# Two readers of a logits bank: the copies and the maxima of a key tile start at different heads

## The chip, the cores and the metric

The kernel runs on one core of a Trainium2 chip. The metric is the device time of one launch in microseconds (us). Before the change it is 3161.52 us, the median of three runs (3156.13 to 3167.02). The engines are named as in the profile: PE is TensorE, PEld its weight loads, DVE VectorE, ACT ScalarE, POOL GpSimd, SP the queue that issues DMAs.

## What is computed

Eight images of 512 channels and 32 x 32 pixels go through a convolutional block with two attention bottlenecks, and then through a grouped 1x1 convolution. Cut to what bears on the change, each of the two bottlenecks of an image does this:

```python
z = cbs(yi, m_cv1_w[i], m_cv1_bn[i], 1)                    # 3x3 convolution, SiLU
q, k, v = conv2d(z, qkv_w, 0) split in three, 4 heads of 64
logits = jnp.einsum('bhdi,bhdj->bhij', q, k + r) * HD ** (-0.5)
a = jax.nn.softmax(logits, axis=-1)                        # over 1024 keys
out = jnp.einsum('bhij,bhdj->bhdi', a, v)
ys.append(yi + silu(bn_eval(conv2d(out, m_cv2_w[i], 0))))
```

Around it stand a GroupNorm and a 1x1 convolution (cv1), a 1x1 convolution over all branches (cv2), and a second GroupNorm with the last layer's 1x1 convolution (l). Everything is float32.

## The kernel before

**Units of attention.** The attention is cut into 64 units, called passes here: image, bottleneck, pair of heads (hp) and half of the 1024 queries. A pass keeps its logits transposed: 128 keys on the partitions, 512 queries along the row, one bank of PSUM for each of the two heads. There are KT = 8 key tiles of 128 keys. The methods of `class Unit` (L493 to L585) are the steps:

- `logits(t)`, L502: two matmuls (L510) fill one bank for each head; ScalarE copies both banks into the SBUF tile `st` (L517); from the second tile on, VectorE keeps a running elementwise maximum `mx` of the tiles (L522). For t = 1 it takes the maximum of the first tile's copy and the second tile's bank, afterwards of `mx` and the bank. The first tile has no maximum.
- `top()` and `spread()`, L524 and L533: PE transposes `mx` (L530), VectorE reduces it to the negated maximum of each query (L531), and PE spreads that over the partitions into `mb` (L539).
- `soften(t)`, L542: VectorE adds `mb` to the logits (L544).
- `exponent(t)`, L546: ScalarE takes the exponential in place (L548); GpSimd adds the tiles up (L555).
- `values(t)`, L557: PE multiplies the exponentials with v into `po` (L562).
- `finish()` and `divide()`, L571 and L581: PE sums over the keys (L576), ScalarE copies the sum out (L579), VectorE takes reciprocals (L583) and multiplies (L585).

**The order.** The loop at L1047 to L1086 runs over the passes and, within a pass, over pairs of key tiles. While pass u is softened, exponentiated and multiplied with v, the logits of the next pass `nxt` are made. For each pair t, t + 1 it writes: `soften` of both; `exponent(t)` (not for t = 0); `values` of the two tiles before; for t = 0 `divide` of the pass before; `nxt.logits` of both tiles; the remaining exponentials. Then `advance` writes filler for PE: convolutions of other stages (cv1, cv2, 3x3 products at L313, the projection qkv, the last layer), with their evictions by ScalarE (L130 for SiLU, L396, L412, L333, L349) and by VectorE (L399, L430, L457, L486).

An engine carries out its instructions in the order in which the build queues them. That order is the program's as far as an instruction is ready in the build's own estimate; three chains fix it further. `act_turn` (L188) chains the copies and the exponentials on ScalarE, `in_turn` (L182) the maxima, the additions of soften and the steps of the 3x3 transform on VectorE, and `pe_turn` (L196) the attention's matmuls on PE. `divide` is in no chain. Semaphores between engines come from the tiles that an instruction reads and writes.

**PSUM.** All logits, fillers and small results take their banks in turn from one pool of five (`ps_f`, L63, tag `bank`); `mb` and `po` have pools of their own. A bank is written again only when both of its readers are done.

Of the kernel before, what the change touches and what calls it, by code (L numbers as in the profile page):

```python
# [17 lines left out]
ALU = mybir.AluOpType  # L18
# [21 lines left out]
def conv_preact_kernel(ctx: ExitStack, tc: tile.TileContext, x, cv1, cv2, mcv1, qkv, mcv2, bn, rw, rh, conv, s_in, t_in, out):  # L40
    nc = tc.nc
# [23 lines left out]
    def pair(p, tag, name):  # L65
        return p.tile([P, 2, HALF], F32, tag=tag, name=name)

    def bank(name):
        return ps_f.tile([P, HALF], F32, tag="bank", name=name)
# [112 lines left out]
    def in_turn(instruction):  # L182

        if turn:
            tc.add_manual_dep(instruction.ins, turn.pop().ins.name, IN_ORDER, reason="order of VectorE")
        turn.append(instruction)

    def act_turn(instruction):  # L188

        if act_last:  # L190
            tc.add_manual_dep(instruction.ins, act_last.pop().ins.name, IN_ORDER, reason="order of ScalarE")
        act_last.append(instruction)
# [3 lines left out]
    def pe_turn(instruction):  # L196

        if pe_last:
            tc.add_manual_dep(instruction.ins, pe_last.pop().ins.name, IN_ORDER, reason="order of TensorE")
        pe_last.append(instruction)  # L200
# [292 lines left out]
    class Unit:  # L493
# [8 lines left out]
        def logits(self, t):  # L502

            if t == 0:
                self.begin()
            lg = [bank(f"lg_{self.name}_{t}_{h}") for h in range(2)]
            for h in range(2):
                r = slice(HD * h, HD * h + HD)
                pe_turn(
                    nc.tensor.matmul(  # L510
                        lg[h], self.k[r, ts(t, P)], self.q[r, self.hp, ts(self.half, HALF)], start=True, stop=True
                    )
                )
            st = pair(stp, "st", f"st_{self.name}_{t}")
            self.st.append(st)
            for h in range(2):
                act_turn(nc.scalar.copy(st[:, h], lg[h]))  # L517
            if t == 1:
                self.mx = pair(one, "mx", f"mx_{self.name}")
            for h in range(2 if t else 0):  # L520
                so_far = self.st[0] if t == 1 else self.mx
                in_turn(nc.vector.tensor_tensor(self.mx[:, h], so_far[:, h], lg[h], ALU.max))  # L522

        def top(self):  # L524

# [625 lines left out]
```

## Time and profile before

| what | value |
|---|---|
| median of 3 runs | 3161.52 us |
| profiled execution, its own time | 3162.82 us |
| span of the profiled execution | 3161.1 us |
| granted clock of TensorE, mean | 0.996 |
| instructions in the span | 34185 |
| DMA | 399.35 MB, 126 GB/s in the mean |
| exponentials L548 on ScalarE | 512, mean 1068 ns |
| additions of soften L544 on VectorE | 512, mean 1215 ns |
| reciprocals L583 on VectorE | 128, mean 1723 ns |
| table loads on ScalarE (L130 and L548) | 223, 1283 ns each |

The profile shows one execution. A group of instructions is a line of the kernel with its engine, operation and tiles; behind it stand the number, the busy time in us, the mean duration of one in ns, and the idle time of the engine just before them with what ended most of it. The waits tell who waited for whom, in us, times and the longest. A wait for several semaphores is put down to the one that came last. In the timeline neighbouring instructions of one line are merged: the first number is the start of the first, the second the time to the end of the last, and a bracket gives the idle time of the engine before and its releaser. "issue" stands for time in which nothing that the profile shows was waited for; for weight loads, most of it is their spacing behind the matmuls.

Outside the attention stages lie the first 174 us (the first convolution and the making of weights) and the last 163 us. From 174 to 2998 us PE is busy for 2770.7 of 2824 us, VectorE for 1910.8 and ScalarE for 1630.7.

### The profile page before, as it was taken

Reading aid. Unit: us, or ns where it says so; the run is one execution under the profiler, and the core shown is the slowest. Engines: PE = TensorE matmul, PEld = TensorE weight load, DVE = VectorE, ACT = ScalarE, POOL = GpSimd, SP = SyncE. Lnnn points to the kernel's source line nnn. Section 1 sums busy time; section 2 is a strip of 40 time slices with the busy share of each in tenths; the row PEclk is TensorE's granted clock in tenths of the full one; section 3 lists DMA queues with packets and bytes.
Section 4 is the critical chain, followed back from the end, with each engine's and each line's share of the span. In section 5 each row is a group of like instructions: output and inputs, shape, how many; then the busy total and the mean of one; then the engine's idle time right before and its main releaser. Section 6 shows DMA issues by size and latency. Waiting matters only on the chain.

```text
span 3161.1 us, 34185 instructions
## 1 busy us (share of the span) xinstructions
PE 3077.0 (97%) x11668; PEld 1515.3 (48%) x11668; DVE 2049.9 (65%) x2718; ACT 1721.0 (54%) x2349; POOL 1398.4 (44%) x1867
## 2 busy tenths in 40 slices
PE   7999999998999999999999999999999999999999
PEld 3645354454445454455445454454445454453333
DVE  5446577567667576667666676767666676767642
ACT  3245765855655555644656455544656455546621
POOL 2104444546444554455444454445444464444520
PEclk9999999999999999999999999999999999999999
DMA  8852352421233232424233332424233332413356
GB/s 289 292 182 74 130 180 87 153 77 63 88 116 131 79 128 71 149 84 148 84 116 130 114 127 70 153 85 136 91 110 130 120 120 70 150 64 120 120 205 217
DMA packets 142014, 399.35 MB, mean 126 GB/s; under 512 B 13072, under 2 KB 14352, under 8 KB 141840
## 3 DMA queue, kind: packets, MB, share of 16 engines
q1 hardware_dynamic: 141120, 396.94, 36.6%
q8 instruction: 92, 1.51, 0.2%
q14 instruction: 82, 0.67, 0.1%
q10 hardware_dynamic: 720, 0.23, 0.0%
HBM read 317.42 MB, written 79.69 MB: 126 GB/s over the span
## 4 chain that ended last, share of the span: by engine, by line
PE 75%; DVE 4%; ACT 4%; issue 2%; DMA 1%; POOL 1%; SPq 0%; ACTq 0%; DVEq 0%; POOLq 0%
PE cv L175 15%; PE m L313 13%; PE po L562 12%; PE lg L510 12%; PE l L175 7%; PE qk L175 6%; PE v L405 3%; PE m L175 3%; PE den L576 2%; PE mb L539 2%; PE mt L530 1%; ACT st L517 1%; DVE st L544 1%; ACT st L548 1%; DVE mx L522 1%
## 5 line engine op out<-in xcount | busy, mean ns | idle before, releaser
L555 POOL TENSOR_TENSOR sum<-sum,st 128x256 f32<-128x256 f32 x1536 | 1132.0, 771 | 552.1 <-ACT st L548 547.7
L522 DVE TENSOR_TENSOR mx<-mx,lg 128x512 f32<-128x512 f32 x768 | 477.8, 682 | 417.6 <-ACT st L517 417.4
L517 ACT COPY st<-lg 128x512 f32<-128x512 f32 x1024 | 525.0, 597 | 356.1 <-PE lg L510 331.7
L548 ACT ACTIVATE st<-st 128x1024 f32<-128x1024 f32 x512 | 539.1, 1068 | 304.1 <-DVE st L544 302.9
L544 DVE TENSOR_TENSOR st<-st,mb 128x1024 f32<-128x1024 f32 x512 | 604.4, 1215 | 60.2 <-PE mb L539 60.2
L555 POOL TENSOR_TENSOR sum<-st,st 128x256 f32<-128x256 f32 x256 | 185.1, 754 | 788.8 <-ACT st L548 788.8
L313 PE MATMUL m<-plane,w_m 128*128 128x256 f32 x2304 | 528.8, 383 | 4.9 <-ACT cv2s L130 2.7
L562 PE MATMUL po<-st,v 128*64 128x512 f32 x2048 | 497.8, 605 | 18.2 <-ACT st L548 16.2
L510 PE MATMUL lg<-q,k 64*128 64x512 f32 x2048 | 510.9, 617 | 2.9 <-ACT y L130 2.9
L313 PEld LDWEIGHTS m<-plane,w_m 128*128 128x128 f32 x2304 | 426.4, 189 | 129.5 <-issue 45.1
L175 PE MATMUL cv<-y,w_cv 128*128 128x512 f32 x1024 | 464.5, 599 | 7.9 <-ACT cv2s L130 4.6
L510 PEld LDWEIGHTS lg<-q,k 64*128 64x128 f32 x2048 | 177.3, 186 | 328.2 <-issue 267.4
L175 PEld LDWEIGHTS cv<-y,w_cv 128*128 128x128 f32 x1024 | 185.8, 190 | 248.1 <-issue 226.4
L562 PEld LDWEIGHTS po<-st,v 128*64 128x64 f32 x2048 | 128.8, 136 | 323.6 <-issue 237.3
L175 PE MATMUL cv<-x,w_cv 128*128 128x512 f32 x512 | 237.0, 610 | 10.6 <-ACT y L130 3.7
L175 PE MATMUL l<-x,w_l 128*128 128x512 f32 x512 | 236.9, 606 | 7.9 <-DVE mx L522 6.9
L175 PE MATMUL qk<-z,w_qkv 128*128 128x512 f32 x512 | 234.0, 600 | 1.4 <-DVE mx L522 1.4
L583 DVE RECIPROCAL rb<-rb 128x256 f32<-128x256 f32 x128 | 215.5, 1723 | 26.0 <-ACT rb L579 25.8
L531 DVE TENSOR_REDUCE nm<-mt 128x4 f32<-128x512 f32 x128 | 82.3, 684 | 144.7 <-PE mt L530 144.7
L579 ACT COPY rb<-den 128x512 f32<-128x512 f32 x64 | 37.3, 583 | 230.4 <-PE den L576 230.4
L175 PEld LDWEIGHTS cv<-x,w_cv 128*128 128x128 f32 x512 | 95.3, 194 | 132.0 <-issue 109.3
L175 PEld LDWEIGHTS l<-x,w_l 128*128 128x128 f32 x512 | 93.4, 191 | 130.4 <-issue 112.2
(145 smaller groups left out, 2408.8 us busy)
## 6 DMA issues: line engine op xcount, KB each, us to landing
w_m<-w_m SPq DMA_DIRECT2D x96, 768.0 KB, 4.8
w_cv<-in_cv SPq DMA_DIRECT2D x90, 512.0 KB, 3.5
y<-y SPq DMA_DIRECT2D x64, 512.0 KB, 4.8
x<-in_x SPq DMA_DIRECT2D x56, 512.0 KB, 5.2
y<-y SPq DMA_DIRECT2D x64, 256.0 KB, 3.5
k<-r SPq DMA_DIRECT2D x32, 512.0 KB, 3.6
res<-y SPq DMA_DIRECT2D x32, 512.0 KB, 4.0
xr<-in_x SPq DMA_DIRECT2D x32, 512.0 KB, 4.1
```

The costliest lines, as they stand in the source:

```text
L175: nc.tensor.matmul(ps, w, moving, start=(n == 0), stop=(n == len(terms) - 1))
L313: nc.tensor.matmul(ps[:, ts(co, 256)].rearrange("p (t x) -> p t x", x=F), w[:, co, c, dx], u[:, 9 * c : 9 * c + 8, dx : dx + F], start=(j ...
L405: nc.tensor.matmul(ps[:, ts(j, P)], z[:, c, ts(4 * j4 + j, P)], w[:, c, 512 + P * hp : 512 + P * hp + P], start=(c == 0), stop=(c == IT - 1),)
L510: nc.tensor.matmul(lg[h], self.k[r, ts(t, P)], self.q[r, self.hp, ts(self.half, HALF)], start=True, stop=True)
L517: act_turn(nc.scalar.copy(st[:, h], lg[h]))
L522: in_turn(nc.vector.tensor_tensor(self.mx[:, h], so_far[:, h], lg[h], ALU.max))
L531: nc.vector.tensor_reduce(self.nm[:, h], mt, AX.X, ALU.max, negate=True)
L544: in_turn(nc.vector.tensor_tensor(st, st, flat(self.mb), ALU.add))
L548: act_turn(nc.scalar.activation(st, st, AF.Exp))
L555: nc.gpsimd.tensor_tensor(flat(self.acc)[:, part], flat(so_far)[:, part], st[:, part], ALU.add)
L562: nc.tensor.matmul(self.po[HD * h : HD * h + HD], self.v[:, t, ts(h, HD)], self.st[t][:, h], start=(t == 0), stop=(t == KT - 1),)
L583: nc.vector.reciprocal(self.rb[:, r], self.rb[:, r])
```

## The change

In `logits(t)` the two copies and the two maxima are written in another order. Before: copy of head 0, copy of head 1, maximum of head 0, maximum of head 1. After: copy of head 0, maximum of head 1, copy of head 1, maximum of head 0. Operands, shapes, numbers of instructions and the chains `act_turn` and `in_turn` are the same; within the chains the maxima of a tile change places. For t = 0 there is no maximum, and the two copies stay as they were.

```diff
             self.st.append(st)
-            for h in range(2):
-                act_turn(nc.scalar.copy(st[:, h], lg[h]))
             if t == 1:
                 self.mx = pair(one, "mx", f"mx_{self.name}")
-            for h in range(2 if t else 0):
-                so_far = self.st[0] if t == 1 else self.mx
-                in_turn(nc.vector.tensor_tensor(self.mx[:, h], so_far[:, h], lg[h], ALU.max))
+            so_far = self.st[0] if t == 1 else self.mx
+
+            def copy(h):
+                act_turn(nc.scalar.copy(st[:, h], lg[h]))
+
+            def greater(h):
+                if t:
+                    in_turn(nc.vector.tensor_tensor(self.mx[:, h], so_far[:, h], lg[h], ALU.max))
+
+            copy(0)
+            greater(1)
+            copy(1)
+            greater(0)
```

## The prediction

> **What bounds the kernel.** I first read the busy times of the page, then its costliest groups, the waits, and the timeline of single passes (one pass is one Unit: 64 passes of eight key tiles).
>
> ```profile
> PE 3077.0 (97%) x11668; PEld 1515.3 (48%) x11668; DVE 2049.9 (65%) x2718; ACT 1721.0 (54%) x2349; POOL 1398.4 (44%) x1867
> ```
>
> TensorE works in 97% of the 3161.1 us span, and the chain that ended last is 75% PE. So an edit pays only if it takes away a stretch in which PE stands still, and costs only if it makes one. VectorE (65%) and ScalarE (54%) have idle time in the mean; what counts is where they are late.
>
> ```profile
> L522 DVE TENSOR_TENSOR mx<-mx,lg 128x512 f32<-128x512 f32 x768 | 477.8, 682 | 417.6 <-ACT st L517 417.4
> L517 ACT COPY st<-lg 128x512 f32<-128x512 f32 x1024 | 525.0, 597 | 356.1 <-PE lg L510 331.7
> ```
>
> A maximum takes 682 ns, a copy 597 ns. VectorE is idle 417.6 us before its maxima, nearly all released by the copies. From the third key tile on, a maximum reads nothing that a copy writes; the two only read the same bank. So the program keeps two reads of one bank apart, in the order in which they are written: copy first, maximum second. The changed kernel will do the same in its own order: head 0 copy, then maximum; head 1 **maximum, then copy**. ScalarE will wait for VectorE, which this trace never shows.
>
> ```profile
> DVE mx L522 <- ACT st L517: 433.2, 174, 9.0
> PEld po L562 <- ACT st L548: 78.0, 92, 4.6
> PE po L562 <- ACT st L548: 16.2, 14, 3.7
> PE cv L175 <- DVE mx L522: 4.1, 5, 1.7
> ```
>
> The waits (us in total, times, longest): the big one is VectorE's and not PE's. PE's waits for a maximum that frees a bank are l 6.9 us, cv 4.1, po 2.0, m 1.6, mt 1.6 and qk 1.4: 17.6 us in 20 waits. PE also waits for the exponentials that feed values().
>
> **The change, part by part.** It adds and removes no instruction: 1024 copies, 896 maxima, the same DMAs. It turns round which engine reads head 1 first, in 448 key tiles (the first tile of a pass has no maximum).
>
> *Step 1, a pair of tiles with VectorE free.* In the pass whose third pair starts at 1220.41 us, the four copies run from 1221.64 to 1223.69 and the four maxima from 1222.26 to 1224.74. Maxima follow each other every 0.60 us, copies every 0.48; a maximum began 0.04 us after the copy it waited for. In the new order, maximum 1 runs beside copy 0, maximum 0 beside copy 1: two slots of 0.60 to 0.72 us a tile; from 1221.64 the maxima end near 1224.16, 0.58 earlier, and the copies and the exponential behind them 0.5 later. The second and the fourth bank are freed 0.58 earlier, the first and third at the old time. For PE this is worth at most 0.58 us in each of the 20 waits, and no more than the wait: l 3x0.58, cv 5x0.58, po 1.7, m 1.6, mt and qk 0.58 each: 9.1 us. Half of the banks gain nothing: I take **-5 us** (0 to -9). That VectorE is done sooner otherwise hides in its idle time.
>
> *Step 2, the second key tile of a pass.* This is the tile with the new wait. Behind spread() VectorE has two additions of soften (2.35 us together), two reciprocals (3.36) and two products (0.69) before it reaches the maxima; PE meanwhile needs about 5 us to the end of the logits. VectorE is late there by construction:
>
> ```profile
> 1241.44 2.35 DVE L544 TENSOR_TENSOR st<-st,mb 128x1024 f32<-128x1024 f32 x2 [0.95 <-PE mb L539]
> ...
> 1243.71 3.36 DVE L583 RECIPROCAL rb<-rb 128x256 f32<-128x256 f32 x2
> 1243.99 1.99 PE L510 MATMUL lg<-q,k 64*128 64x512 f32 x8
> 1245.21 2.05 ACT L517 COPY st<-lg 128x512 f32<-128x512 f32 x4 [2.20 <-PE lg L510]
> 1245.91 1.98 PE L175 MATMUL cv<-y,w_cv 128*128 128x512 f32 x4
> 1246.99 0.69 DVE L585 TENSOR_TENSOR q<-po,rb 128x256 f32<-128x256 f32 x2
> 1247.12 2.03 ACT L548 ACTIVATE st<-st 128x1024 f32<-128x1024 f32 x2
> 1247.59 1.28 DVE L522 TENSOR_TENSOR mx<-st,lg 128x512 f32<-128x512 f32 x2
> 1248.26 2.02 PE L562 MATMUL po<-st,v 128*64 128x512 f32 x8 [0.37 <-ACT st L548]
> ```
>
> (Columns: start, us from first start to last end, engine and line.) ScalarE does its four copies without a wait, the last from 1246.64, and goes on to the two exponentials, which PE's values() is already waiting for. In the changed kernel the last copy waits for maximum 1, which can't start before 1247.59: it ends 0.69 later, 1248.28, and the copy starts near 1248.32, **1.68 us late**. Behind it in ScalarE's queue stand exactly those exponentials, and behind them PE's values matmuls, then everything else on PE. This pass loses 1.7 us.
>
> I did this subtraction for the second tile of each of the 63 passes after the first, from the timeline: (start of the first maximum + 0.73) - (start of the last copy), less ScalarE's idle time before the exponential. The exponentials become late by 100 us in all, 1.6 in the mean. What covers it is PE's filler between the logits and values(): the time by which an exponential is done before its values matmul. In **17 passes** there is none (0.05 to 0.1 us, as above): delays of 0.35 to 1.7, sum 24.7 us. In **9 more** the delay exceeds a cover of 1.6 to 1.9 us (six with a delay of 3.4, as after 1503.68 us, where the copies are done at 1506.96, the first maximum starts at 1509.01 and values() at 1510.94; there 1.8 us remain), and in a tenth 4.7 exceeds 3.1: together 14.4 us. In the other **36** it is hidden by filler matmuls; were that filler gone they would pay their 0 to 2.8 us. Sum **+39 us**. Bounds: 0 if something hides all, +100 if nothing is hidden.
>
> *Step 3, later tiles.* In 28 of 192 later pairs VectorE is busy elsewhere when the first copy ends; the copies then end 1 to 4 us late, in the rest 0.5. Their exponentials have mostly 2 to 13 us in hand; five pairs have less than their delay: **+3 us** (0 to +6). ScalarE's evictions of PE's other banks (L130, L396, L412) stand behind the late copies as well. PE's own waits for L130 are now 17 us in 14 waits; half a microsecond more on each, roughly half of it real: **+4 us** (0 to +15).
>
> *Step 4, what comes back.* Where PE is made late, its own later waits in the pass shrink. PE's waits outside start-up, tail and exponentials add up to 42 us; 27 of 63 passes hold some 18 of them: I take **-7 us** (0 to -18).
>
> The Trainium skill, "PSUM — Partial Sum Buffer", section "Specifications (TRN2)", says that ScalarE and VectorE read PSUM in parallel at full bandwidth so long as their banks differ. By that rule alone the change would only gain, Step 1's 5 us. The same page's "Engine vs sequencer instructions" calls the ScalarE and VectorE queues strict FIFO; by that rule the exponentials can't pass the waiting copy, and Step 2 stands. The timeline above shows the order that this rule needs, and it shows no copy that waits for a maximum.
>
> **Sum.** 39 + 3 + 4 - 5 - 7 = +34 us. The profiled execution took 3162.82 us (span 3161.1), so 3196.8; the median of the runs is 1.3 lower: **3195.5 us**.
>
> **Rivals.**
> *A, the wait is larger.* If the passes with 1.6 us of cover lose it too (their delays are 1.0 to 1.5, so it takes 0.2 to 0.7 us of extra lateness), and evictions cost their upper bound, then 39 + 15 + 6 + about 15 = +75: 3236 us. For: some fifteen passes sit just inside. Against: ScalarE is idle for 46% of the span and catches up within a pass.
>
> *B, hidden.* Divide() has no written turn on VectorE. If the build, seeing ScalarE idle, fills it with evictions or lets PE's filler go ahead of values(), half of Step 2 goes: +10 to +18, 3172 to 3180 us. Against: in 248 of 256 places logits follow values directly, as written.
>
> *C, faster.* One mechanism: maximum 1 no longer needs copy 0, so the build could place it ahead of the reciprocals. If it is placed before the second one (1.7 us earlier), the last copy is no longer late, Step 2 falls to nothing and Step 1's gain stays, 5 us by my value and 17.6 if all waits of PE for a maximum go: 3144 to 3157 us. It decides once maxima start within 1 us of the end of the logits. Against: the logits end 2 us after the first reciprocal starts, and both reciprocals are written earlier and ready earlier.
>
> *D, the change does nothing,* if banks were not what orders the reads. The 417.4 us released by copies speak against it; 3161.5 us.
>
> **How the numbers follow.** Forecast (3180 to 3215) 0.58, A (above 3215) 0.14, B (3165 to 3180) 0.13, C 0.11, D 0.04. A measurement of this kernel can tell 0.3% from no change, that is 3152.0 and 3171.0. Faster: the lower part of C, 0.07. Same: the rest of C (0.04), D, and the third of B below 3171 (0.05): 0.13. Slower 0.80. The range takes in B, D and A's priced value and leaves out C and what is above A: 3158 to 3238.
>
> **What will show it.** Right: ScalarE idle before its copies, released by mx, 150 to 250 us (100 from Step 2, half a microsecond for each later pair); VectorE's 417.6 us before the maxima more than halved; PE busy unchanged near 3077, and its waits of po for ScalarE's exponentials up by 30 to 45 us. Wrong: divide() behind the maxima in the second tile (C); po waits as before (B); or PE waits that grow mainly at evictions (A).

## The result and the profile after

The changed kernel takes 3213.45 us (median of 4 runs, 3206.39 to 3217.47) against 3158.82 us for the kernel before on the same chips: 54.6 us more, a ratio of 1.0167 with a 95% interval of [1.015, 1.0183]. The forecast was slower, by 34 us, with a range up to 3238. Side and range held; the size was 20 us short. The profiled execution took 3216.37 us (span 3214.7), 53.6 more than that of before. In the changed kernel a copy is L521, a maximum L525, soften L553, the exponential L557, values() L571.

From the page of the changed kernel (busy us and share; then line, engine, operation, busy and mean ns, idle time and its releaser):

```profile
PE 3099.8 (96%) x11668; PEld 1521.5 (47%) x11668; DVE 2056.0 (64%) x2718; ACT 1749.4 (54%) x2345; POOL 1384.1 (43%) x1867
...
L521 ACT COPY st<-lg 128x512 f32<-128x512 f32 x1024 | 562.2, 587 | 555.2 <-PE lg L510 295.7
L525 DVE TENSOR_TENSOR mx<-mx,lg 128x512 f32<-128x512 f32 x768 | 488.2, 682 | 382.1 <-PE lg L510 317.2
```

The work is the same: 11668 matmuls, 2718 VectorE instructions, and durations of 587 and 682 ns for copy and maximum (597 and 682 before). ScalarE's idle time before its copies has grown from 356.1 to 555.2 us. VectorE's before its maxima is only a little smaller, but it now ends mostly with the logits (317.2 us) and not with a copy.

The waits of the changed kernel (engine and line, what it waited for, us in all, times, longest):

```profile
DVE mx L525 <- PE lg L510: 317.2, 127, 6.6
...
ACT st L521 <- DVE mx L525: 151.6, 242, 4.5
...
ACT st L521 <- POOL sum L564: 94.4, 42, 4.4
DVE mx L525 <- ACT st L521: 75.6, 62, 8.5
...
PE po L571 <- ACT st L557: 58.8, 36, 5.3
```

The copies now wait 151.6 us for maxima, a row that the trace of before does not have; the maxima wait 75.6 instead of 433.2 us for copies. PE's own wait for the exponentials has gone from 16.2 to 58.8 us. Before, 2.0 us more of it stood under the maxima's name (the row of `po` and `mx`; the swapped maxima below show why), so it grew by **40.6 us**. That is where the time went first. A second row grew that the prediction did not name: the copies wait 94.4 us (24.2 before) for GpSimd's sums, which hold the ten `st` tiles that the copies write.

The pass that the prediction worked through (its logits of the second tile ended at 1245.98 us before) looks like this in the changed kernel, in the timeline of PE, ScalarE and VectorE:

```profile
1267.21 1.99 PE L510 MATMUL lg<-q,k 64*128 64x512 f32 x8
1269.13 3.70 PE L175 MATMUL cv<-y,w_cv 128*128 128x512 f32 x8
1273.12 2.02 PE L571 MATMUL po<-st,v 128*64 128x512 f32 x8 [0.29 <-ACT st L557]
```

```profile
1268.42 1.56 ACT L521 COPY st<-lg 128x512 f32<-128x512 f32 x3 [2.20 <-PE lg L510]
1271.52 0.58 ACT L521 COPY st<-lg 128x512 f32<-128x512 f32 x1 [1.53 <-DVE mx L525]
1272.01 2.95 ACT L557 ACTIVATE st<-st 128x1024 f32<-128x1024 f32 x3
```

```profile
1266.93 3.36 DVE L592 RECIPROCAL rb<-rb 128x256 f32<-128x256 f32 x2
1270.21 0.69 DVE L594 TENSOR_TENSOR q<-po,rb 128x256 f32<-128x256 f32 x2
1270.81 1.27 DVE L525 TENSOR_TENSOR mx<-st,lg 128x512 f32<-128x512 f32 x2
```

The last copy stands apart from the other three: it starts at 1271.52, when the first maximum (1270.81, behind reciprocals and products) has ended. From the end of the logits (1269.20) to values() it is 3.92 us, before it was 2.28: 1.64 more, where the prediction had 1.68. Yet PE idles here for only 0.29 us: eight filler matmuls instead of four now stand before values(). The build had moved filler into this pass, and it is missing elsewhere.

A pass with no filler at all between the logits and values() shows the rest of the price. Two stretches of the changed kernel (us, busy time of PE, PEld, DVE, ACT and POOL, then granted clock, DMA), PE's timeline there, and the values matmuls of the same pass before:

```profile
735.00:741.00 6.00, 2.15 (x10) 0.69 (x8) 6.00 (x7) 3.08 (x6) 0.00 (x0) 0.86 0.00 0
741.00:746.00 5.00, 4.92 (x12) 1.53 (x14) 2.35 (x3) 1.91 (x3) 3.95 (x6) 0.50 0.00 0
```

```profile
735.17 1.99 PE L510 MATMUL lg<-q,k 64*128 64x512 f32 x8
741.08 3.68 PE L571 MATMUL po<-st,v 128*64 128x512 f32 x8 [3.92 <-ACT st L557]
744.69 2.70 PE L510 MATMUL lg<-q,k 64*128 64x512 f32 x8
```

```profile
728.28 2.02 PE L562 MATMUL po<-st,v 128*64 128x512 f32 x8 [2.28 <-ACT st L548]
```

PE idles 3.92 us for the exponentials, 1.64 more than before. The granted clock falls within this stall, at 739.3 us, and is **0.50** from 741 to 746 us: the eight values matmuls take 3.68 us where before they took 2.02, the eight logits matmuls 2.70 where the pass above shows 1.99. The stall is paid a second time, as busy time of PE. The view of the cores gives the mean granted clock of the span:

```profile
core 0: 3214.7 us, clock 0.991
```

0.009 of 3214.7 us is 29 us of full-speed time lost; before, at 0.996 of 3161.1 us, it was 13. The stretches at half clock themselves (58 us against 27, in the last section) give half of 31, some 15 us. But a part of them lies where PE stands idle and loses nothing, as from 739.3 to 741.08 us above. PE is busy for 49 us of them, for 24 before; half of this difference, some **12 us** of the 53.6, are clock.

### The profile page after: what moved, and what is told of

The parts are those of the page before. It is cut to its first block, busy times and chain, and to the rows that moved or that the text cites. A ratio compares the mean times of both kernels' runs of the same rounds, so it can differ in the third digit from the quotient of the medians.

```text
span 3214.7 us, 34240 instructions
## 1 busy us (share of the span) xinstructions
PE 3099.8 (96%) x11668; PEld 1521.5 (47%) x11668; DVE 2056.0 (64%) x2718; ACT 1749.4 (54%) x2345; POOL 1384.1 (43%) x1867
## 4 chain that ended last, share of the span: by engine, by line
PE 78%; DVE 9%; ACT 6%; issue 3%; DMA 3%; POOL 0%; SPq 0%; ACTq 0%; DVEq 0%; POOLq 0%
PE cv L175 16%; PE m L313 15%; PE lg L510 12%; PE po L571 11%; PE qk L175 7%; PE l L175 7%; PE v L405 4%; DVE st L553 2%; ACT st L557 2%; PE mt L539 2%; DVE rb L592 2%; PE mb L548 2%; DMA x<-in_x 1%; DVE mx L525 1%; ACT st L521 1%
## 5 line engine op out<-in xcount | busy, mean ns | idle before, releaser
L564 POOL TENSOR_TENSOR sum<-sum,st 128x256 f32<-128x256 f32 x1536 | 1117.8, 762 | 559.7 <-ACT st L557 559.7
L521 ACT COPY st<-lg 128x512 f32<-128x512 f32 x1024 | 562.2, 587 | 555.2 <-PE lg L510 295.7
L525 DVE TENSOR_TENSOR mx<-mx,lg 128x512 f32<-128x512 f32 x768 | 488.2, 682 | 382.1 <-PE lg L510 317.2
L553 DVE TENSOR_TENSOR st<-st,mb 128x1024 f32<-128x1024 f32 x512 | 603.8, 1214 | 64.3 <-PE mb L548 64.2
L557 ACT ACTIVATE st<-st 128x1024 f32<-128x1024 f32 x512 | 532.5, 1057 | 161.9 <-DVE st L553 160.5
L571 PE MATMUL po<-st,v 128*64 128x512 f32 x2048 | 508.8, 614 | 59.0 <-ACT st L557 58.8
L510 PE MATMUL lg<-q,k 64*128 64x512 f32 x2048 | 521.1, 621 | 1.2 <-ACT y L130 1.2
L571 PEld LDWEIGHTS po<-st,v 128*64 128x64 f32 x2048 | 127.7, 137 | 371.8 <-issue 214.2
L175 PEld LDWEIGHTS qk<-z,w_qkv 128*128 128x128 f32 x512 | 92.3, 190 | 127.3 <-issue 95.8
```

Of the source, the lines that this page charges most:

```text
L175: nc.tensor.matmul(ps, w, moving, start=(n == 0), stop=(n == len(terms) - 1))
L510: nc.tensor.matmul(lg[h], self.k[r, ts(t, P)], self.q[r, self.hp, ts(self.half, HALF)], start=True, stop=True)
L553: in_turn(nc.vector.tensor_tensor(st, st, flat(self.mb), ALU.add))
L557: act_turn(nc.scalar.activation(st, st, AF.Exp))
L564: nc.gpsimd.tensor_tensor(flat(self.acc)[:, part], flat(so_far)[:, part], st[:, part], ALU.add)
L571: nc.tensor.matmul(self.po[HD * h : HD * h + HD], self.v[:, t, ts(h, HD)], self.st[t][:, h], start=(t == 0), stop=(t == KT - 1),)
```

## Experiments: which tile pays

"Before" is the kernel before in runs on the same chip. The diffs are against the changed kernel, where nothing else is said.

### New order in the second tile only, and in the later tiles only

```diff
-            copy(0)
-            greater(1)
-            copy(1)
-            greater(0)
+            if t == 1:
+                copy(0)
+                greater(1)
+                copy(1)
+                greater(0)
+            else:
+                copy(0)
+                copy(1)
+                greater(0)
+                greater(1)
```

In the second kernel the condition is `t > 1`.

> New order in the second key tile of each pass only; later tiles as before. Theory (ScalarE's last copy waits there for VectorE, which is late by its reciprocals): nearly the whole loss is here. PE idle before the values matmuls of the first tile as in the changed kernel, 40 to 48 us against 14.5 before; the last copy of the second tile later by about 100 us summed over 63 passes; time +35 to +50 us over before. Rival (the loss comes from ScalarE being half a microsecond late in every later pair, through evictions and buffers): +0 to +12 us.

> New order from the third key tile on; the second tile as before. Theory: PE idle before the first tile's values matmuls back near 15 us; a few late exponentials of later tiles remain, and the banks come free earlier: -5 to +12 us against before. Rival (every later pair costs): +35 to +50 us.

Measured: second tile only 3205.46 us against 3156.05, ratio 1.0156 [1.0143, 1.017], **+49.4 us**. Later tiles only 3162.26, ratio 1.0016 [1.0007, 1.0024], **+6.2 us**. The two add up to 55.6, the whole change to 54.6. The rival by which every later pair costs is out: 64 of the 448 copies that now stand behind a maximum carry nine tenths of the loss. The last copy of the second tile, summed over 63 passes from the timeline, starts 131 us after the first copy of its tile (30 us before), and PE's idle time ahead of the first tile's values matmuls is 42.8 us (14.5 before). PE's row of the first kernel, and two rows of the second:

```profile
PE po L577 <- ACT st L563: 48.1, 31, 5.3
```

```profile
PE po L577 <- ACT st L563: 14.1, 12, 3.7
PE po L577 <- DVE mx L525: 8.9, 10, 2.3
```

The second kernel's two rows are both waits for exponentials, as the next experiment shows. Of their 23.0 us, 14.6 lie ahead of the first tile's values matmuls, as before.

### Only the maxima change places

```diff
             copy(0)
-            greater(1)
             copy(1)
+            greater(1)
             greater(0)
```

A second kernel swaps the maxima in the second tile alone; its other tiles have the old order.

> Both copies first, as before, then the maximum of head 1, then that of head 0: the same new order of the maxima, but no copy waits for a maximum. Theory: ScalarE never waits for VectorE, so the time is that of before within 0.3% (0 to +8 us, since the first bank is freed later). Rival (the order in which the build queues other work behind the swapped maxima makes the loss): +20 us and more.

> Second tile: both copies first, then the maximum of head 1, then of head 0; all else as before. It splits the swapped maxima's cost by tile. If the first bank's later release counts mostly where VectorE is late, in the second tile: +6 to +14 us over before, as with all tiles swapped. If it is spread over all tiles: 0 to +3 us.

Measured, all tiles swapped: 3170.55 us against 3156.05, ratio 1.0043 [1.0029, 1.0056], **+14.5 us**. That is more than the first theory allowed (0 to +8), and less than its rival's +20. No copy waits for a maximum here, and the exponentials are as early as before. PE's waits for banks tell it:

```profile
PE cv L175 <- DVE mx L525: 8.0, 7, 2.8
PE m L313 <- DVE mx L525: 8.0, 13, 0.9
PE po L571 <- DVE mx L525: 7.7, 9, 2.3
PE l L175 <- DVE mx L525: 6.9, 4, 2.8
```

The rows of cv, m and l have 22.9 us, against 12.6 before; with the smaller rows it is 24.2 against 15.6: 9 more. PE takes its banks in turn, and the bank it takes first is now read last. The row of `po` is no wait for a bank of the logits, since `po` has a pool of its own: PE's idle times of 1.11 and 2.28 us ahead of the first tile's values matmuls at 550 and 729 us, which this trace puts down to maxima, are there before as well, with the same lengths and put down to exponentials. In the profiled executions PE's idle time is 8 us longer than before and its busy time 4 us; what the latter comes from is open. With the second tile alone swapped it is 3154.48 us against 3159.01, ratio 0.9987 [0.9978, 0.9996]: not slower but 4.5 us faster. Both halves of the expectation missed: the second tile gains a little, and if the two parts add up, the cost of the swap is in the later tiles (no run swaps those alone). Why the second tile gains is open; its clock (0.998) is better than that of before, and the build queues some other work differently. For the case at hand one thing is settled: the 49 us of the second tile do not come from the order of its maxima, but from the copy that stands behind one.

### Taking away what makes VectorE late

```diff
         def divide(self, part):
             r = ts(part, HALF // 2)
-            nc.vector.reciprocal(self.rb[:, r], self.rb[:, r])
```

The same line is left out of both kernels.

> The kernel before with the 128 reciprocals of divide left out (the quotients are replaced by products). It takes 3.4 us per pass off VectorE just ahead of the second tile's maxima. Both theories: 0 to -15 us against before, since PE is the bound; this is the reference for the next run.

> The changed kernel with the same reciprocals left out. Theory (the last copy of the second tile is late because VectorE stands in its reciprocals): the delay of that copy falls from 133 us summed to 60 or less, PE's idle time before the first tile's values matmuls from 44 to below 22 us, and the time lies only 0 to +15 us above the kernel before without reciprocals. Rival (any wait of ScalarE for VectorE costs so much, whatever stands ahead): +40 to +55 us above it.

Measured: the kernel before without reciprocals 3157.42 us against 3159.01, ratio 0.9999 [0.9988, 1.001], so these 215 us of VectorE's time are worth nothing to it. The changed kernel without them: 3165.27, ratio 1.0016 [1.0007, 1.0025], **+7.9 us** over the other where the full kernels differ by 54.6. The second tile's last copy starts 62 us behind its first, summed (133 with the reciprocals, 30 in the old order), and PE idles 17.6 us ahead of the first tile's values matmuls (44.4). The waits of ScalarE and PE:

```profile
ACT st L521 <- PE lg L510: 316.1, 143, 5.6
ACT st L521 <- POOL sum L564: 94.3, 36, 4.4
ACT st L521 <- DVE mx L525: 91.4, 237, 4.9
```

```profile
PE po L571 <- ACT st L557: 28.5, 19, 4.1
```

The copies still wait 91.4 us for maxima, and 94.3 us for GpSimd's sums as in the full change, and the former in nearly as many places (237, 242 in the full change). So the wait as such is cheap. What costs is that in the second tile it is a wait for an engine with a fixed backlog, ahead of the exponentials that PE needs next. What is left has the size of one thing: PE's idle time ahead of the later tiles' values matmuls, 10.9 us against 2.3 in the kernel before without reciprocals.

### Is the clock part of it?

```diff
             if t == 0:
                 self.po = ps_o.tile(...)
+                idle = {1: 7, 6: 5, 7: 20, 11: 17, ...}.get(units.index(self), 0)
+                if idle:
+                    spare = bank(f"spare_{self.name}")
+                    for j in range(idle):
+                        pe_turn(nc.tensor.matmul(spare[:, ts(j % 4, P)], ident, ones, start=True, stop=True))
```

The numbers are those of the passes where PE stood idle for over 1 us. In a second kernel the same lines are added to the kernel before, with that kernel's passes.

> The changed kernel with 177 small matmuls that nobody reads (128x128, 0.22 us each by the transposes' rows) put ahead of the first tile's values matmuls in the 19 passes where PE stood idle there for over 1 us, no more than that idle time. They add work and no use. Theory that the half-clock stretches after PE's idle time are a part of the loss: stretches at half clock fall from 60 us to 25 to 45, and the time falls by 5 to 15 us against the changed kernel (ratio to before 1.012 to 1.015). Rival (the clock is not part of it): the time is that of the changed kernel or up to 10 us more.

> The kernel before with 46 unread matmuls of 0.22 us in the six passes where PE stood idle for 1.1 to 3.7 us ahead of the first tile's values matmuls. Theory (half-clock stretches cost time in the kernel before as well): of its 30 us at half clock 7 to 14 go, and the time falls by 2 to 6 us. Rival (no part of the clock is to be had here): 0 to +5 us.

Measured on the changed kernel: 3199.7 us against 3159.01, ratio 1.0128 [1.0114, 1.0142]. The unfilled one has 1.0167 [1.015, 1.0183]. Useless work made it about 0.4%, **12 us**, faster. The second tile's last copies and the exponentials are as late as without it (132 and 233 us, summed as above; 133 and 234 in the changed kernel), so the stall's cause is untouched; but the granted clock is back:

```profile
core 0: 3192.8 us, clock 0.998
```

0.002 of the span is 6 us lost instead of 29: by that account up to 23 us were to be had, and the one profiled execution is 22 us shorter than the other (3194.56, the fastest of its four, against 3216.37). On the kernel before, 46 such matmuls in six passes changed nothing that can be measured: 3160.88 against 3158.22, ratio 1.0006 [0.9996, 1.0015], clock 0.997. The expected 2 to 6 us did not come; the stalls there are few, and other stretches at half clock remained.

### Maxima from the copies

```diff
-                    in_turn(nc.vector.tensor_tensor(self.mx[:, h], so_far[:, h], lg[h], ALU.max))
+                    new = st[:, h] if t == 1 else lg[h]
+                    in_turn(nc.vector.tensor_tensor(self.mx[:, h], so_far[:, h], new, ALU.max))
```

With maxima that read the copy in SBUF, no logits bank depends on VectorE. The first kernel does so in the second tile (later tiles in the new order), the second in all tiles (old order), the third like the second with the second tile's maxima swapped.

> Second tile: both copies first, and the maxima read the copies in SBUF instead of the banks, so that the banks depend on ScalarE alone; later tiles in the new order. Theory: no copy of the second tile waits for VectorE and its banks are free some 1 to 3 us earlier: as in the kernel with the new order in the later tiles only, or up to 8 us less; the 128 maxima may take longer than 0.68 us, as VectorE operations on SBUF alone show 0.86 us, which costs VectorE 23 us that PE does not see. Rival (VectorE's load itself holds PE): +5 to +20 us over that kernel.

> Old order, but every maximum reads the copy in SBUF instead of the bank, so that all logits banks depend on ScalarE alone. If banks that come free late are worth PE time: PE's 17.6 us of waits for maxima go and the time is 5 to 12 us under before. Rival (the maxima get longer on SBUF alone, 0.71 us for the second tile's and up to 0.86 us where GpSimd is busy, and VectorE's later work moves back): same as before within 0.3% or up to 10 us slower.

> As the kernel with all maxima from the copies, with the second tile's maxima swapped. If the gain of that swap (about 4 us) came from the banks' order, it is gone here, since no bank depends on a maximum: equal to the kernel without the swap within 2 us. If it comes from the order of other work in the build: another 2 to 6 us less.

Measured: 3163.99 us against 3156.05, ratio 1.0028 [1.0017, 1.0039], that is 1.7 us above the kernel with the new order in the later tiles alone: no gain from the earlier banks. All tiles: 3227.73 against 3158.22, ratio 1.0226 [1.021, 1.0241], **+69.5 us**, far outside what either theory allowed. With the swap 3227.3, the same. The groups of VectorE and GpSimd in the second kernel show it:

```profile
L525 DVE TENSOR_TENSOR mx<-mx,st 128x512 f32<-128x512 f32 x768 | 714.7, 987 | 345.3 <-ACT st L521 345.1
```

```profile
L564 POOL TENSOR_TENSOR sum<-sum,st 128x256 f32<-128x256 f32 x1536 | 1338.6, 905 | 471.1 <-ACT st L557 470.9
```

A maximum takes 987 ns in the mean instead of 682, and a sum 905 instead of 771: both engines lose. Taken one by one in this trace, the later tiles' maxima that run wholly beside GpSimd's work take 1158 ns and those beside none 685; in the kernel before both take 682. Of the second tile's 128 maxima, 116 run beside none, before the sums of the pass have begun, and take 683. PE's idle time is 125 us instead of 84, and none of the growth lies ahead of values() (18.7 and 18.1 us): it is spread over waits for evictions, banks and the other steps behind the two engines. The Trainium skill, "SBUF — State Buffer", section "Who interferes with whom", says that a VectorE instruction with two SBUF inputs contends with a GpSimd instruction that reads SBUF; these rows agree with it. The page's "Summary: rules for kernel authors" adds that the second of the two to issue blocks fully until the first finishes; the rows show means of 1.45 and 1.17 times the old durations, and can't tell how that is divided.

## Why the prediction was right, and where it was short

**The bound** (PE; only its stretches of standing still count): right for VectorE, where 215 us less work changed nothing in the old order. But a stall also lengthened PE's busy time behind it, which "costs only if it makes one" leaves out.

**Step 1** (banks free earlier, -5 us, bounds 0 to -9): right, and near the upper bound. PE's waits for maxima and for copies that free a bank were 16.5 us (15.6 and 0.9) and are 8.2 in the changed kernel (0.9 and 7.3): 8 us less. The prediction's 17.6 us and 20 waits hold 2.0 us in three waits of `po`, which were waits for exponentials (the swapped maxima show it), so its bound of 9.1 is 1.7 too high. The new order in the later tiles alone was +6.2 us all the same, so this gain is more than given back there.

**Step 2** (second tile, +39 us): the mechanism and the arithmetic hold. The exponentials were to be late by 100 us in all; their start after the end of the logits grew from 131 to 234 us, by **102**. The stretch from the logits to values() was to grow by 39; it grew from 305 to 344 us, by **39**. Nor is that luck in the sum: in the 17 passes without cover it grew by 27 us (24.7 forecast), in the ten with too little by 13.5 (14.4), in the 36 others it shrank by 2 (0). The term's error is in what PE does in that stretch: its idle time grew by 30 us (14.5 to 44.4) and not by 39, since in nine of the 17 passes the build put more filler there. That is a little of rival B. With the second tile alone in the new order and with the reciprocals left out, the cause is shown, not only argued.

**Step 3**: two errors. The later tiles' exponentials were given +3 us with a bound of 6; PE's idle time ahead of the later tiles' values matmuls grew from 3.7 to 14.4 us, **+10.7**, beyond that bound. In the prediction only VectorE made copies late; in the changed kernel they wait 70 us more for GpSimd's sums, which hold the `st` tiles. Late exponentials would make late sums, and those late copies. That this is the cause of the 10.7, or the whole of it, is not shown: no run takes the wait for the sums away. The evictions were given +4; PE's waits for L130 fell from 17 to 13 us.

**Step 4 with Steps 1 and 3's evictions**: -8 in the sum; PE's waits outside start-up, tail and exponentials went from 41 to 31 us, -10 (the prediction's 42 hold the 2 us of `po`).

**The missing term.** The sum has no row for the clock. The granted clock was on the page's line and in the windows of before (0.996, and 0.99 and 0.98 outside the attention stages), but each microsecond of stall was priced at one microsecond. With 30 + 10.7 - 10 + 12 = 43 us the four measured terms cover most of the profiled 53.6. Without the 12 of the clock they give 31, near the forecast; that nearness is luck in part, since Step 2 came out 9 lower and the exponentials of Step 3 8 higher. Some 11 us stay without a name: PE's busy time grew by 22.8 us, of which 12 are clock.

**Rivals.** A (above 3215 us) did not come about, though the time is nearly there: not by the passes with 1.6 us of cover and not by evictions, but by the clock and the later tiles. B shows in single passes only. C, reciprocals behind the maxima, did not happen: VectorE's order in the pass above is the old one. D is out. The prediction's "ScalarE will wait for VectorE, which this trace never shows" holds for the copies alone: the exponentials waited 302.9 us for VectorE's additions before.

**What was to show it**: ScalarE's wait for maxima 150 to 250 us, measured 151.6; po's waits up by 30 to 45, measured 42.6 by their row and 40.6 with the 2 us of the other name; PE busy unchanged near 3077, wrong: 3099.8. VectorE's idle time before maxima more than halved, wrong: 417.6 to 382.1. Its wait for copies did fall from 433.2 to 75.6, but the engine had nothing else to do and waits for the logits instead.

## What to carry to other kernels

Where two engines read the same bank, the order in which the reads are written decides who waits for whom. Let the engine whose queue holds the critical work go first, and make the one with the backlog wait: here two kinds of instruction changed places, nothing was added, and it cost 1.7%. Count such a wait at the place where the backlog is fixed (here behind two reciprocals), not as a mean over all tiles. And price a stall of PE of about two or more microseconds higher than its length, by the clock that the trace shows after such stalls.

## What was not expected of the hardware

- **Half clock after short stalls.** The trace's record of the granted clock has, besides the ends, six stretches of 3.4 or 6.8 us at 0.50 before (27 us) and twelve after (58 us). All but the first of each, near 88 us, overlap gaps of PE of 1.8 us or more or follow them within 1.2 us; in the kernel with the new order in the later tiles one follows a single gap of 2.0 us. The Trainium skill, "TensorE: Matmul & The Clock Gate", section "HAM oscillation — how this bites in real kernels", gives as an abstract rule that gaps over about 3.4 us are to be avoided; here gaps of 1.8 to 2.9 us were enough in several places, while others of that length passed without it.
- **Where a gap falls decides.** In each of the 13 traces the half-clock stretches begin whole multiples of 3.413 us apart, to within 0.01 us. Cut into windows on that grid, from 20 us on, the traces show 81 windows at full clock in which PE is idle for 60% or more: every one is followed by half clock. Of some 11,800 windows that are idle for less than half none is, but for the one near 88 us in 11 of the traces, after a window of busy PE; between, 13 of 42 are. So before, a gap of 2.13 us that fills 62% of one window (607.5 to 610.9 us) is followed by half clock, and in the changed kernel one of 2.86 us that is split into 42% and 42% of two (at 1454.7 us) is not.
- **Work that nobody reads can save time**: 177 small matmuls in PE's idle stretches brought the clock from 0.991 to 0.998 and took about 12 us off.
- **VectorE and GpSimd on SBUF**: a maximum of 682 ns with one operand in PSUM took 987 ns with both in SBUF beside GpSimd's sums, and those went from 771 to 905 ns.
- **The fastest of the orders tried** is the one with the second tile's maxima swapped behind both copies, 0.9987 [0.9978, 0.9996] of before; it is under the 0.3% that one comparison here can tell, and its cause is open.
